# Four graph layers on one core: row sums of the adjacency matrix by four column quarters of TensorE, and one chain of roots for twelve tiles

## The chip, the cores and the metric

The kernel runs on one core of a Trainium2 chip. The time is device microseconds of that core for one launch; lower is better. The times given are medians of several executions; the profile is that of one more execution.

## What is computed

Four graph layers follow each other on x (2708 x 512) with one adjacency matrix adj (2708 x 2708, some 0.6% of it filled, and a filled diagonal). The first one, cut from the reference:

```python
h = jnp.maximum(_layernorm(x, axis=-1), 0.0)
deg = jnp.sum(adj_matrix, axis=1)
dinv = (deg + 1.0) ** (-0.5)
aug = dinv[:, None] * (adj_matrix + jnp.eye(n)) * dinv[None, :]
x = x + jax.nn.relu(aug @ h @ weight)
```

The second layer uses (deg + 1e-8) ** -0.5 without the added unit matrix, the third again the form of the first, and the fourth an attention over the neighbours. So before the first product can be scaled, the row sums deg of all of adj that belong to a tile of h must be known, with the root of deg + 1 and the mean and variance of the tile's rows of x.

## The kernel before, in words

The matrix arrives transposed, so that deg is a sum over columns' partitions: a sum down the 128 partitions of each block. Its rows and columns are cut into four quarters of 677. Each quarter has five full tiles of 128 rows; what is left (37 rows of each quarter) is gathered in two tail tiles, so there are NT = 22 tiles, of which NF = 20 are full. A block is yb[j, q, u]: the 5 x 128 full rows of quarter j by one half (u, 339 columns) of quarter q. It is 128 x 1695 f32 in SBUF, 847.5 KB. yt holds the tail rows.

The products adj @ h are done by a Winograd-like scheme on two levels: outer_product and multiply take sums and differences of blocks (DVE additions of 128 x 1695) and of halves of h, so that seven products do the work of eight. multiply (L446) runs products pa, pb, pc, pd of five matmuls each (L454) into PSUM banks; inner_x (L405) makes the sums s1 to s4 of h, and inner_y (L421, additions L428 to L431) those of the blocks.

The first layer (first_aggregate, L585) does this while the degrees are made. Its order:

- Two tail loads (L592), then four pieces (q, u) in degrees (L281). Each loads two blocks of the lower half of the matrix (L286, into one of three places, `early`) and two of the upper half that are kept for the product (L289), adds the first two on DVE (L290), adds the unit matrix's diagonal to the kept block (add_loops, L389), and sums columns on PE with column_sums (L254): the stationary operand is one column of ones, and the moving one 128 x 339 of a block, so that one partition of PSUM takes the sums (15 matmuls, L258, and two for the tails in tail_sums_of, L251 and L252). ACT copies the row of sums out (L261).
- After the second piece of a quarter, quarter_h (L263) cuts the two rows of sums into tiles' columns and first_h (L324) turns them into columns: a matmul each (L330) with the 128 numbers as stationary operand and a single one as moving operand. Then come the roots: rsqrt (L179) is a square root on ACT, a reciprocal and four small DVE instructions that refine it, once for the degree and once for the variance; then ACT normalizes five tiles (L211).
- h of quarters 0 and 1 (XA, XB) now stands, and the first product p1 runs for both halves u. Meanwhile DVE makes sums of blocks for later products (third_sums L622, second_sums L629) that GpSimd writes to DRAM (keep_o, L376).
- The degrees of quarters 2 and 3 come in other_degrees (L298), from block sums that the product makes anyway, before each half of product 7. Their tiles' x is loaded late (L653), and their statistics (first_stats, L657) and roots follow: a chain of roots for quarter 2, one for quarter 3, and one for each of the two tail tiles (tail_degrees, L314).
- Then h of the quarters 2 and 3 is subtracted (by_halves, L662; minus_sum, L399) and the product of the next kind begins. other_roots (L340) makes the second layer's roots five tiles at a time.

The order of the instructions on each engine isn't that of the source alone: a list scheduler of the framework interleaves them, within the dependencies, when the program is built. Each engine then takes its own in order. SP issues the loads in order and waits, with all behind it, where a place isn't free. PSUM has five banks for the products (`ps_agg`), two for `ps_out`, one for `ps_sm`.

Of the kernel before, what the change touches and what calls it, by code (L numbers as in the profile page):

```python
# [8 lines left out]
FP = mybir.dt.float32  # L9
AF = mybir.ActivationFunctionType  # L10
ALU = mybir.AluOpType
# [26 lines left out]
def gnn_kernel(  # L38
# [40 lines left out]
        nc.vector.tensor_add(again_ident, again_ident, ident[:, k * G : (k + 1) * G])  # L79
    ones = const.tile([P, P], FP, name="ones")  # L80
    nc.vector.memset(ones, 1.0)
    bab = const.tile([P, 2], FP, name="bab")
    nc.gpsimd.dma_start(bab[:, 0:1], ba.partition_broadcast(P))
    nc.gpsimd.dma_start(bab[:, 1:2], bb.partition_broadcast(P))
# [52 lines left out]
    def take(places):  # L137

        places.append(places.pop(0))
        return places[-1]  # L140
# [13 lines left out]
    def repeat(g, n):  # L154

        while n < P:
            nc.vector.tensor_copy(g[..., n : 2 * n], g[..., 0:n])
            n *= 2
# [17 lines left out]
        return [g[:, c] for c in range(len(cs))]  # L176


    def rsqrt(o, v, n):  # L179

        s = small.tile([P, KT], FP, tag="rs", name="rs")
        nc.scalar.activation(s[:, :n], v, AF.Sqrt)
        nc.vector.reciprocal(o, s[:, :n])
        q = small.tile([P, KT], FP, tag="rq", name="rq")
        nc.vector.tensor_mul(q[:, :n], o, o)
        nc.vector.tensor_mul(q[:, :n], q[:, :n], v)
        nc.vector.tensor_scalar(q[:, :n], q[:, :n], -0.5, 1.5, ALU.mult, ALU.add)
        nc.vector.tensor_mul(o, o, q[:, :n])
# [4 lines left out]
        nc.vector.bn_aggr(mv, st)  # L193

    def rstd_of(mv, n):
        v = small.tile([P, KT], FP, tag="rv", name="rv")
        nc.vector.tensor_scalar(v[:, :n], mv[:, :n, 1], LN_EPS, None, ALU.add)
        rstd = small.tile([P, KT], FP, tag="rstd", name="rstd")
        rsqrt(rstd[:, :n], v[:, :n], n)
        return rstd  # L200

    def shift_of(mv, scale, n):

        b = small.tile([P, KT], FP, tag="sh", name="sh")
        nc.vector.scalar_tensor_tensor(
            b[:, :n], mv[:, :n, 0], -1.0, scale[:, :n], ALU.mult, ALU.mult
        )
        return b
# [25 lines left out]
            stats(h[:, t, :], mv0[:, t, :])  # L234


    left = ends[0:1, 4 * BLK : ENDS]
    acct = left[:, 2 * W : 2 * W + NQ * (R0 + R1)].rearrange("p (q r) -> p q r", q=NQ)
    parts = {(0, u): left[:, u * W : (u + 1) * W] for u in range(U)}
    parts[1, 0] = between[0:1, 3 * BLK : 3 * BLK + W]  # L240

    def load_tails(q, u, tl=None):
        if tl is None:
# [2 lines left out]
            nc.sync.dma_start(tl[:, s, :], yt[s, :, q, u])  # L246
        return tl

    def tail_sums_of(ps, tls):

        nc.tensor.matmul(ps[0:1], ones[:, 0:1], tls[0], start=True, stop=False)  # L251
        nc.tensor.matmul(ps[0:1], ones[:G, 0:1], tls[1], start=False, stop=False)  # L252

    def column_sums(ps, blocks, to):  # L254

        last = KT * len(blocks) - 1
        for n in range(last + 1):
            nc.tensor.matmul(  # L258
                ps[0:1], ones[:, 0:1], blocks[n // KT][:, n % KT, :], start=False, stop=n == last
            )  # L260
        nc.scalar.copy(to, ps[0:1])  # L261

    def quarter_h(q, two):  # L263

        nc.vector.tensor_copy(acct[:, q, :], two[1][:, KT * P - W : Q - W])
        across = small.tile([1, P], FP, tag="across", name="across", bufs=1)
        k = W // P
        nc.vector.tensor_copy(across[:, 0 : W - k * P], two[0][:, k * P : W])
        nc.vector.tensor_copy(across[:, W - k * P : P], two[1][:, 0 : (k + 1) * P - W])

        def columns(t):
            o = (t % KT) * P
            if t % KT == k:
                return across
            return two[0][:, o : o + P] if t % KT < k else two[1][:, o - W : o - W + P]

        first_h(list(range(q * KT, (q + 1) * KT)), columns)

    y11 = {}

    def degrees(q, u, ps):  # L281


        two = [take(early) for _ in range(2)]
        for k in range(2):
            nc.sync.dma_start(two[k], yb[2 + k, q, u])  # L286
        for j in (q, 1 - q):
            y11[j, q, u] = blk = free.pop(0)
            nc.sync.dma_start(blk, yb[j, q, u])  # L289
        nc.vector.tensor_add(two[0], two[0], two[1])  # L290
        add_loops(y11[q, q, u], u, 1)
        column_sums(ps, [two[0], y11[q, q, u], y11[1 - q, q, u]], parts[0, u])

    def tail_place(b, u):

        return agg[:, 1, 1, :, b, u * W : (u + 1) * W]

    def other_degrees(u, ys):  # L298

        if u == 0:  # L300
            parts[1, 1] = upool.tile([P, W], FP, tag="s", name="row")[0:1]
        for b, blocks in ((0, (ys[1], ys[2])), (1, (ys[7],))):
            ps = ps_out.tile([P, W], FP, tag="out", name="dg_ps")
            tl = tail_place(b, u)
            tail_sums_of(ps, (tl[:, 0], tl[:G, 1]))
            column_sums(ps, blocks, parts[b, u])
        if u < U - 1:
            return
        for b in range(2):
            quarter_h(2 + b, [parts[b, v] for v in range(U)])  # L310
        tail_degrees(NF)
        tail_degrees(NF + 1)

    def tail_degrees(t):  # L314
        o, m = (0, R0) if t == NF else (R0 - PAD, R1P)
        g = small.tile([1, P], FP, tag="dt", name="dt", bufs=1)
        nc.vector.tensor_scalar(
            g[:, 0 : NQ * m].rearrange("p (q r) -> p q r", q=NQ), acct[:, :, o : o + m],
            1.0, None, ALU.add,
        )  # L320
        repeat(g, NQ * m)
        first_h([t], lambda t: g)

    def first_h(ts, columns):  # L324

        n, t0 = len(ts), ts[0]
        span = slice(t0, t0 + n)
        pd = ps_sm.tile([P, KT], FP, tag="sm", name="pd")
        for s, t in enumerate(ts):
            nc.tensor.matmul(pd[:, s : s + 1], columns(t), ones[0:1, 0:1], start=True, stop=True)  # L330
        nc.vector.tensor_copy(deg[:, span], pd[:, :n])
        rsqrt(dinv[:, span], deg[:, span], n)
        mv = mv0[:, span, :]
        rstd = rstd_of(mv, n)
        nc.vector.tensor_mul(rstd[:, :n], rstd[:, :n], dinv[:, span])
        sh = shift_of(mv, rstd, n)
        for s, t in enumerate(ts):
            normalized(t, h[:, t, :], rstd[:, s : s + 1], sh[:, s : s + 1])

    def other_roots():  # L340

        nc.vector.tensor_scalar(deg, deg, 1.0, 1e-8, ALU.subtract, ALU.add)
        for t in range(0, NT, KT):
            n = min(KT, NT - t)
            rsqrt(dis[:, t : t + n], deg[:, t : t + n], n)

# [236 lines left out]
    def first_aggregate(epilogue):  # L585
# [2 lines left out]
        free += more  # L588
        spare = [block(later_h, k * BLK) for k in range(3)]
        tls = [tpool.tile([P, KT, W], FP, tag="t", name=f"tails{s}") for s in range(2)]  # L590
        for s in range(2):
            nc.sync.dma_start(  # L592
                tls[s][:, 0 : 2 * U], yt[s, :, 0:2].rearrange("p q u w -> p (q u) w")
            )
        pieces = [(q, u) for q in range(2) for u in range(U)]
        ps = {a: ps_agg.tile([P, W], FP, tag="agg", name="dg_ps") for a in pieces}
        for q, u in pieces:
            tail_sums_of(ps[q, u], (tls[0][:, q * U + u], tls[1][:G, q * U + u]))
        for q, u in pieces:
            degrees(q, u, ps[q, u])  # L600
            ts = range(q * KT, (q + 1) * KT)
            if u == 0:
                first_x(ts)
                first_stats(ts)
            else:
                quarter_h(q, [parts[0, v] for v in range(U)])
            if (q, u) == (1, 0):
                ys = inner_y([y11[a, b, u] for a, b in QUAD], u, 0, own_t3)
        blks = {u: [y11[a, b, u] for a, b in QUAD] for u in range(U)}
# [4 lines left out]
        p1, p7 = (0, 0, "as it is"), (1, 1, "as it is")  # L614
        for u in range(U):
            for b in range(2):
                load_tails(2 + b, u, tail_place(b, u))
        xs_ = inner_x(XA)
        multiply(xs_, ys, 0, [p1])
        ys = inner_y(blks[1], 1, 0, own_t3)  # L620
# [341 lines left out]
    def attention(t, columns):  # L962
        xt = load_x(t, xs)
        y = load_x(t, xbs)
        nc.scalar.activation(xt, xt, AF.Copy, bias=0.5)
        sm = ps_sm.tile([P, KT], FP, tag="sm", name="pse")
        nc.tensor.matmul(sm[:, 0:1], columns(t), ones[:, 0:1], start=True, stop=True)
        pE, _ = project(wsa_sb, t)
        g = small.tile([P, 1], FP, tag="ge", name="ge")
        nc.vector.tensor_add(g, sm[:, 0:1], eps[:, t : t + 1])  # L970
        nc.vector.reciprocal(g, g)
        nc.vector.tensor_mul(g, g, ga[:, t, 0:1])
        nc.vector.scalar_tensor_tensor(y, pE, g, y, ALU.mult, ALU.add)
        nc.scalar.activation(y, y, AF.Tanh, scale=0.5)
        nc.vector.scalar_tensor_tensor(xt, y, 0.5, xt, ALU.mult, ALU.add)
        for o, n, to in place(t):
            nc.gpsimd.dma_start(out[to : to + n, :], xt[o : o + n, :])
# [140 lines left out]
```

## Time and profile before

| | |
|---|---|
| median of 3 runs | 2152.46 us (2147.79 to 2152.94) |
| the profiled execution, its own time | 2149.36 us |
| its span, first to last instruction | 2147.6 us |
| mean granted TensorE clock | 0.994 |
| PE busy | 2100.2 us (98%), 7270 matmul passes |
| DVE busy | 1448.8 us (67%), 2573 instructions |
| ACT, POOL busy | 385.8 us (18%), 171.1 us (8%) |
| moved by DMA | 359.10 MB, mean 167 GB/s |

Each f32 matmul stands as two records (passes) in the trace, each with its weight load. A busy PE is a PE that has a matmul in its pipe, not one at its peak. The whole span is:

```profile
PE   8999979999999999999999999999999999999998
DVE  4799857567666867777576869968537755666512
DMA  8894596445554444654453656554542233233212
```

One digit is the busy share, in tenths, of a fortieth of the span (53.7 us). The parts that the change touches lie in the first four digits.

The sums of columns have two neighbours in the trace. First, the single column of ones: weight loads of 128 x 1 take 79 to 128 ns, matmuls of 128 x 339 446 to 451 ns from start to end. Second, the transposing matmuls (L330): 245 ns, with weight loads of 181 to 187 ns, 44 in number (22 tiles, two passes).

### The profile page before, as it was taken

The numbers are of one execution on the slowest core, as the hardware profiler recorded it, in microseconds if no ns is written. First come the engines' busy times: TensorE is split into PE (matmuls) and PEld (weight loads), VectorE is DVE, ScalarE is ACT, GpSimd is POOL, SyncE is SP. The second block draws the span as 40 slices with busy tenths as digits, with TensorE's granted clock in tenths as the row PEclk, the third lists the DMA queues.
The fourth block names the chain that finished last, engine by engine and source line by source line (L and its number), as shares of the span: only waits on it lengthen the run. The fifth ranks groups of instructions, "written<-read, shape, count | busy, mean of one in ns | idle before, by whom it ended". The sixth has DMA issues, their size and how long they took to land.

```text
span 2147.6 us, 19913 instructions
## 1 busy us (share of the span) xinstructions
PE 2100.2 (98%) x7270; PEld 1288.8 (60%) x7270; DVE 1448.8 (67%) x2573; ACT 385.8 (18%) x765; POOL 171.1 (8%) x314
## 2 busy tenths in 40 slices
PE   8999979999999999999999999999999999999998
PEld 2556646556666645566664546666677666666664
DVE  4799857567666867777576869968537755666512
ACT  1121000222000010100001121000116534444401
POOL 0000010211000020200001130000001000000001
PEclk9999989999999999999999999999999999999999
DMA  8894596445554444654453656554542233233212
GB/s 334 322 357 166 181 304 200 163 148 201 177 169 166 154 152 153 227 171 156 162 176 127 220 196 205 173 162 158 192 163 75 97 101 101 94 101 100 80 41 65
DMA packets 79201, 359.10 MB, mean 167 GB/s; under 512 B 10540, under 2 KB 14892, under 8 KB 79104
## 3 DMA queue, kind: packets, MB, share of 16 engines
q1 hardware_dynamic: 51584, 252.02, 34.4%
q0 software_dynamic: 27520, 105.82, 14.6%
q8 instruction: 57, 0.93, 0.2%
q14 instruction: 40, 0.33, 0.0%
HBM read 295.65 MB, written 62.15 MB: 167 GB/s over the span
## 4 chain that ended last, share of the span: by engine, by line
PE 52%; issue 33%; DVE 7%; DMA 6%; POOL 2%; ACT 1%; POOLq 0%; SPq 0%; DVEq 0%; ACTq 0%
PE pa L454 10%; PE pd L454 9%; PE pc L454 9%; PE po L734 6%; PE pb L454 5%; PE pe L1025 4%; PE pg L873 3%; PE pt L505 2%; PE dg_ps L258 2%; DMA ends<-xs 1%; POOL ends L741 1%; DMA obuf<-in_yb_dram 1%; DMA obuf<-osumt 1%; PE pt L510 1%; DVE ends L826 1%
## 5 line engine op out<-in xcount | busy, mean ns | idle before, releaser
L1025 PE MATMUL pe<-obuf,h 128*128 128x339 f32 x1280 | 372.9, 448 | 0.0
L454 PE MATMUL pa<-obuf,h 128*128 128x339 f32 x1050 | 321.4, 450 | 3.1 <-ACT h L211 1.6
L1025 PEld LDWEIGHTS pe<-obuf,h 128*128 128x128 f32 x1280 | 240.9, 189 | 126.6 <-issue 10.0
L734 PE MATMUL po<-ends,agg 128*128 128x512 f32 x640 | 281.4, 596 | 1.8 <-ACT ends L754 1.5
L454 PEld LDWEIGHTS pa<-obuf,h 128*128 128x128 f32 x1050 | 198.6, 190 | 108.8 <-issue 7.5
L734 PEld LDWEIGHTS po<-ends,agg 128*128 128x128 f32 x640 | 119.6, 190 | 144.6 <-issue 137.7
L454 PE MATMUL pd<-obuf,s 128*128 128x339 f32 x550 | 168.6, 453 | 14.5 <-DVE agg L471 14.4
L946 ACT ACTIVATE e<-r,nsr 128x339 f32<-128x339 f32 x352 | 170.8, 566 | 28.0 <-DVE obuf L950 11.6
L454 PE MATMUL pc<-t,h 128*128 128x339 f32 x560 | 169.4, 448 | 2.9 <-DVE u L492 2.9
L454 PE MATMUL pb<-t,s 128*128 128x339 f32 x560 | 169.9, 448 | 0.2 <-DVE s L399 0.2
L454 PE MATMUL pd<-t,s 128*128 128x339 f32 x560 | 169.2, 448 | 0.0
L482 ACT COPY v<-pa 128x339 f32<-128x339 f32 x56 | 24.6, 440 | 746.3 <-PE pa L454 709.9
L454 PEld LDWEIGHTS pd<-obuf,s 128*128 128x128 f32 x550 | 104.9, 191 | 69.9 <-DVE agg L471 17.0
L454 PEld LDWEIGHTS pc<-t,h 128*128 128x128 f32 x560 | 105.8, 189 | 57.9 <-DVE u L492 4.5
L454 PEld LDWEIGHTS pd<-t,s 128*128 128x128 f32 x560 | 105.9, 189 | 54.3 <-issue 0.5
L454 PEld LDWEIGHTS pb<-t,s 128*128 128x128 f32 x560 | 105.4, 189 | 54.5 <-DVE s L399 0.7
L454 PE MATMUL pc<-obuf,s 128*128 128x339 f32 x450 | 136.1, 448 | 0.0
L454 PEld LDWEIGHTS pc<-obuf,s 128*128 128x128 f32 x450 | 85.2, 189 | 43.7 <-issue 0.5
L429 DVE TENSOR_TENSOR t<-obuf,t 128x1695 f32<-128x1695 f32 x55 | 105.5, 1918 | 0.0
L430 DVE TENSOR_TENSOR t<-obuf,t 128x1695 f32<-128x1695 f32 x53 | 101.6, 1917 | 0.0
L760 POOL DMA_DIRECT2D xs<-ends x66 | 35.9, 543 | 818.3 <-DVE ends L759 757.1
L1042 DVE COPY agg<-pe 128x339 f32<-128x339 f32 x16 | 7.5, 506 | 138.2 <-PE pe L510 138.2
(232 smaller groups left out, 2321.5 us busy)
## 6 DMA issues: line engine op xcount, KB each, us to landing
obuf<-in_yb_dram SPq DMA_DIRECT2D x131, 847.5 KB, 4.5
obuf<-osumt SPq DMA_DIRECT2D x100, 847.5 KB, 4.5
osumt<-obuf POOLq DMA_DIRECT2D x23, 847.5 KB, 9.1
xs<-ends POOLq DMA_DIRECT2D x66, 256.0 KB, 2.3
ends<-xs POOLq DMA_DIRECT2D x66, 256.0 KB, 3.4
obuf<-in_yt_dram SPq DMA_DIRECT2D x32, 339.0 KB, 3.6
agg<-in_yb_dram SPq DMA_DIRECT2D x12, 847.5 KB, 11.3
ends<-in_yb_dram SPq DMA_DIRECT2D x11, 847.5 KB, 8.5
```

The lines of the kernel that those rows point to most:

```text
L258: nc.tensor.matmul(ps[0:1], ones[:, 0:1], blocks[n // KT][:, n % KT, :], start=False, stop=n == last)
L429: nc.vector.tensor_add(t2, o22, t1)
L430: at_t4.append(nc.vector.tensor_add(t4, o21, t2).ins)
L454: nc.tensor.matmul(ps, xs_[q][:, k, :], ys[q][:, k, :], start=start and k == 0, stop=k == KT - 1, skip_group_check=not start,)
L482: nc.scalar.copy(v, pa)
L505: nc.tensor.matmul(ps[c], h[:, NF, c * P : (c + 1) * P], tl[:, 0, :], start=start, stop=False)
L510: nc.tensor.matmul(ps[c], h[g, NF + 1, c * P : (c + 1) * P], tl[g, 1, :], start=False, stop=True)
L734: nc.tensor.matmul(po, cs[c], w_sb[:, c, :], start=(c == 0), stop=(c == NC - 1))
L760: nc.gpsimd.dma_start(xs[t], xt)
L873: nc.tensor.matmul(pk, cs[c], wg_sb[:, c, k, :], start=(c == 0), stop=(c == NC - 1))
L946: nc.scalar.activation(e[:, k], row, AF.Exp, bias=nsr[:, t, s : s + 1], scale=1.0)
L1025: nc.tensor.matmul(pe[c], h[:, t, c * P : (c + 1) * P], a, start=(t == 0), stop=False)
```

## The change

The column sums are made in four column quarters of PE: matmul n of a piece uses columns 32 (n mod 4) and on, with a stationary operand `first` of 128 x 32 (a first column of ones, the rest zero), and writes its own 32 partitions of the bank. So four partial sums stand in partitions 0, 32, 64 and 96, with zeros between. ACT copies all 128 partitions, and the transposing matmul, with 128 ones as moving operand, adds the four. The tails count as two more moving operands, and the second one is filled up with zeros to 128 partitions.

degrees sums all four blocks straight: the DVE addition of two blocks is gone, five more matmuls a piece come in. The diagonal is added to the block after it has been summed, so the degree gets its 1 in first_h. The places for blocks that are only summed are six instead of three (`spare + early`). The loads of tails are one call each (load_rows), the second of 32 rows.

other_degrees collects the columns of quarters 2 and 3 and of both tails and calls first_h once, for twelve tiles: one pair of roots instead of four. other_roots makes one root of 22 columns instead of five. Scratch for roots of more than five columns is hd and eps, which the kernel has for the last layer.

In the built program the scheduler places some things anew. On PE, the five first matmuls of p1 (pa, quarter 0) stand among the sums of piece (1,0), and the transposing matmuls of the twelve tiles stand between the fifth and the sixth of the second half of product 7's seven groups (pa, pb, pa, pc, pd, then pc, pd). On DVE, the chain of roots of the twelve tiles is spread between the additions of blocks L428 to L431, L471 and L703. After about 200 us of the program the order is the same on PE, DVE and SP.

```diff
+    first = const.tile([P, 32], FP, name="first")
+    nc.vector.memset(first, 0.0)
+    nc.vector.memset(first[:, 0:1], 1.0)
...
+    def small_cols(tag, n):
+
+        if n <= KT:
+            return small.tile([P, KT], FP, tag=tag, name=tag)
+        k = ("rs", "rq", "rv", "rstd", "sh").index(tag)
+        return hd[:, :, k] if k < 4 else eps
+
     def rsqrt(o, v, n):
 
-        s = small.tile([P, KT], FP, tag="rs", name="rs")
+        s = small_cols("rs", n)
...
-    def tail_sums_of(ps, tls):
-
-        nc.tensor.matmul(ps[0:1], ones[:, 0:1], tls[0], start=True, stop=False)
-        nc.tensor.matmul(ps[0:1], ones[:G, 0:1], tls[1], start=False, stop=False)
-
-    def column_sums(ps, blocks, to):
-
-        last = KT * len(blocks) - 1
-        for n in range(last + 1):
-            nc.tensor.matmul(
-                ps[0:1], ones[:, 0:1], blocks[n // KT][:, n % KT, :], start=False, stop=n == last
-            )
-        nc.scalar.copy(to, ps[0:1])
...
+    def load_rows(a, b, rows):
+
+        nc.gpsimd.memset(b, 0.0)
+        nc.sync.dma_start(a, rows[0])
+        nc.sync.dma_start(b[:G], rows[1, :G])
+
+    def column_sums(ps, tls, blocks, to):
+
+
+        ops = tls + [blk[:, k, :] for blk in blocks for k in range(KT)]
+        for n, y in enumerate(ops):
+            g = slice(n % 4 * 32, n % 4 * 32 + 32)
+            nc.tensor.matmul(ps[g], first, y, start=n < 4, stop=n >= len(ops) - 4)
+        nc.scalar.copy(to, ps)
...
-    def degrees(q, u, ps):
-
-
-        two = [take(early) for _ in range(2)]
+    def degrees(q, u, ps, tls, places):
+
+        blocks = [take(places) for _ in range(2)]
         for k in range(2):
-            nc.sync.dma_start(two[k], yb[2 + k, q, u])
+            nc.sync.dma_start(blocks[k], yb[2 + k, q, u])
         for j in (q, 1 - q):
             y11[j, q, u] = blk = free.pop(0)
             nc.sync.dma_start(blk, yb[j, q, u])
-        nc.vector.tensor_add(two[0], two[0], two[1])
+            blocks.append(blk)
+        column_sums(ps, tls, blocks, parts[0, u])
         add_loops(y11[q, q, u], u, 1)
-        column_sums(ps, [two[0], y11[q, q, u], y11[1 - q, q, u]], parts[0, u])
...
         for b in range(2):
-            quarter_h(2 + b, [parts[b, v] for v in range(U)])
-        tail_degrees(NF)
-        tail_degrees(NF + 1)
...
+            columns.update(quarter_columns(2 + b, [parts[b, v] for v in range(U)]))
+        columns.update((t, tail_columns(t)) for t in (NF, NF + 1))
+        first_h(columns, NF - half)
...
+    def first_h(columns, looped):
+
+        ts = list(columns)
         n, t0 = len(ts), ts[0]
         span = slice(t0, t0 + n)
-        pd = ps_sm.tile([P, KT], FP, tag="sm", name="pd")
+        pd = ps_sm.tile([P, NT], FP, tag="sm", name="pd")
         for s, t in enumerate(ts):
-            nc.tensor.matmul(pd[:, s : s + 1], columns(t), ones[0:1, 0:1], start=True, stop=True)
-        nc.vector.tensor_copy(deg[:, span], pd[:, :n])
+            nc.tensor.matmul(
+                pd[:, s : s + 1], columns[t], ones[:, 0:1], start=True, stop=True
+            )
+        if looped:
+            nc.vector.tensor_copy(deg[:, t0 : t0 + looped], pd[:, :looped])
+        if looped < n:
+            nc.vector.tensor_scalar(
+                deg[:, t0 + looped : t0 + n], pd[:, looped:n], 1.0, None, ALU.add
+            )
...
-        for t in range(0, NT, KT):
-            n = min(KT, NT - t)
-            rsqrt(dis[:, t : t + n], deg[:, t : t + n], n)
+        rsqrt(dis, deg, NT)
...
+        places = spare + early
         for q, u in pieces:
-            tail_sums_of(ps[q, u], (tls[0][:, q * U + u], tls[1][:G, q * U + u]))
-        for q, u in pieces:
-            degrees(q, u, ps[q, u])
+            ps = ps_agg.tile([P, W], FP, tag="agg", name="dg_ps")
+            degrees(q, u, ps, [tl[:, q * U + u] for tl in tls], places)
             ts = range(q * KT, (q + 1) * KT)
             if u == 0:
                 first_x(ts)
                 first_stats(ts)
             else:
-                quarter_h(q, [parts[0, v] for v in range(U)])
+                first_h(quarter_columns(q, [parts[0, v] for v in range(U)]), 0)
```

## The prediction, made before the changed kernel ran

> **What bounds the kernel now.** I read the page, then the busy time in stretches of the first 300 us (the change touches nothing later), then the column sums' tile, then the timeline and the chain of waits where they stand. Table by stretch (PE, weight loads, DVE, ACT, POOL busy us; granted clock; DMA share; GB/s):
> ```profile
> 10.00:15.00 5.00, 5.00 (x9) 0.33 (x8) 1.79 (x1) 0.00 (x0) 0.00 (x0) 1.00 1.02 427
> ...
> 20.00:25.00 5.00, 5.00 (x18) 1.42 (x17) 3.50 (x9) 0.00 (x0) 0.00 (x0) 1.00 0.97 366
> 25.00:30.00 5.00, 2.73 (x12) 1.02 (x11) 2.80 (x7) 0.43 (x1) 0.00 (x0) 1.00 1.03 430
> 30.00:35.00 5.00, 5.00 (x13) 1.26 (x12) 0.65 (x3) 0.00 (x0) 0.00 (x0) 0.66 0.60 231
> ...
> 75.00:80.00 5.00, 5.00 (x19) 3.28 (x18) 4.43 (x4) 0.00 (x0) 0.00 (x0) 1.00 0.00 1
> ...
> 130.00:140.00 10.00, 10.00 (x35) 4.58 (x34) 10.00 (x9) 2.45 (x1) 0.82 (x2) 1.00 1.02 418
> ```
> In the first 65 us PE, the DMA engines and DVE take turns: transfers run at about 425 GB/s where nothing holds them, and dip (231) where SP waits for one of three places for blocks. From 92 to 150 us PE, DMA and DVE are all full. That matters most: there, time taken off PE alone buys nothing.
>
> The column sums, by tile:
> ```profile
> L258 PE MATMUL dg_ps<-obuf,ones x90: 446/447/451, 20.5 to 142.9; 128*1 128x339 f32 x90
> L258 PE MATMUL dg_ps<-agg,ones x50: 446/448/773, 15.3 to 112.3; 128*1 128x339 f32 x50
> L258 PE MATMUL dg_ps<-ends,ones x40: 446/447/450, 60.0 to 147.1; 128*1 128x339 f32 x40
> ```
> Each f32 matmul is two records: 180 records, 90 matmuls. 447 ns is latency; the pace is 2.86 us for 10 records, 0.286 us a pass, 0.572 us a matmul.
>
> PE's timeline around the end of the stage, and around the next product that DVE feeds:
> ```profile
> 60.01 3.02 PE L258 MATMUL dg_ps<-ends,ones 128*1 128x339 f32 x10
> ...
> 67.93 4.75 PE L454 MATMUL pa<-obuf,h 128*128 128x339 f32 x10 [1.61 <-ACT h L211]
> ...
> 175.45 1.98 PE L454 MATMUL pa<-obuf,h 128*128 128x339 f32 x6 [0.94 <-ACT v L482]
> 177.27 3.02 PE L454 MATMUL pb<-t,s 128*128 128x339 f32 x10
> ```
> So 67.93 us (first product of both quarters) and 177.27 us (first product after the second roots) are the two posts against which I measure. From 177 to 290 us PE is without a gap, and its order and DVE's after about 205 us are the same in both kernels: what is gained at 177.27 is gained at the end. The 12.4 us wait near 290 us is a chain of loads and accumulating transfers started by earlier PE events; it shifts with them.
>
> **Stage 1, to 67.93 us: removed, added, moved.** Removed: four block additions on DVE (L290, 1.93 us each) that PE waited for. Added: 5 more matmuls a piece, 22 instead of 17, on four column quarters. No row shows column quarters. The nearest row is four row groups in tail_products:
> ```profile
> 310.09 0.85 PE L510 MATMUL pt<-obuf,h 32*128 32x339 f32 x8
> 310.87 2.55 PE L505 MATMUL pt<-obuf,h 128*128 128x339 f32 x8
> ```
> Four f32 matmuls (8 passes) take 310.09 to 310.87, 0.78 us instead of 2.29. The Trainium skill, "TensorE: Matmul & The Clock Gate", Part 3, gives three column tiles 2.38 times one; as an estimate that is 0.72 us for three. By the row a piece is 5.5 rounds x 0.78 = 4.3 us, by the page 22/3 x 0.72 = 5.3 us; before 17 x 0.572 = 9.7 us. Bounds: 0.57 us a round (perfect), 2.29 (no overlap). I take 0.78, or 1.3 at the half clock that idle PE gets (0.66 in the 30:35 row): 7.2 us a piece. A rule that speaks against: "TensorEngine Tiling (Array Packing)", Key Properties, says that changing the tiling mode drains the array. The row prices it: from the last full-array start to the row groups' first, and back, the step is about 0.09 us longer than 0.286. Some 26 switches are 2.3 us if all lay on the path; most lie in waits, so I count none here.
>
> Either price is below a piece's loads: four blocks of 847.5 KB, 3.47 MB, 8.2 us at 425 GB/s. So the transfers bound. To the last block of piece (1,1) there are 13.9 MB of blocks, 2.6 of x, 0.9 of tails, 17.4 MB. Before moved 2.2 MB by 10 us (rows 209 and 222 GB/s); the same start, then 425 GB/s, gives 10 + 15.2/0.425 = 45.8 us. Six places instead of three mean that SP no longer waits while the queue empties: only the seventh and eighth block reuse a place, whose sums are done near 20 us while the queue is filled to beyond 35. The zeroing of the second tail block on POOL (128x1356; a 128x128 memset takes 0.20 us, so 0.2 to 2.1 us) holds SP with x and the later blocks behind it until about 5 us, under 8 us of queued blocks: nothing; uncovered, 2 us. The four smaller memsets stand ahead of POOL's first write, near 87 us: nothing. The eight block loads behind piece (1,1) on SP go partly to its first places, read by about 43 us, before the queue runs empty. ACT's copies grow from 1 to 128 partitions: 0.43 us, as L482's 128x339 (0.44); the transposing matmuls likewise: nothing.
>
> Then: sums of the last two blocks, 2.5 rounds, 2.0 to 3.3 us: 48.5 us. DVE is later. Piece (0,1) has landed by 10 + (9.1 - 2.2)/0.425 = 26.3 us and is summed by 28.3; copies, transposing products, the activation table's load (1.28 us) and the roots, some 5 us, let quarter 0 be normalized from 33.4 to 37.0. In PE's new order five matmuls of the first product stand among the sums of (1,0) and wait for this, and ten sums behind them: PE is at 38.6 us when the block that DVE's diagonal additions wait for has been read (before, they went ahead of the sums). Queued behind these on DVE: four additions of 1.85 us and five tiles of statistics (0.78 each), the next diagonal and the copies: 38.6 + 0.65 + 7.4 + 3.9 + 1.3 = 51.9 us. I take 51.9. From the last such copy (63.67) to the product were 4.26 us. So 56.1 instead of 67.93: **-11.8 us**. Bounds: -16 (DMA and PE alone), -7 (everything at half clock, 380 GB/s).
>
> **Stage 2, the sums of the other quarters.** They take PE 5.8, 2.95 and, with the transposing matmuls, 12.5 us (106.90 to 112.70, 116.33 to 119.28, 136.19 to 148.70), 21 us; after, 2 x 5 rounds x 0.78, plus the 12 small products and switches, about 10. **PE gets 11 us, and I credit none of them.** Transfers saturated from 92 us and DVE full from 80 start with the first products, so they move by 11.8 us and no more: x's second half lands at 147.4 - 11.8 = 135.6 us, and the last statistics, with some 0.7 us of root instructions gone from between, end at 152.5 - 12.5 = 140.0. PE will stand instead, near 138 to 142 us, as the twelve columns' products are queued on PE ahead of the last two products and wait for DVE's copies.
>
> **Stage 3, one chain of roots.** Removed: of four chains three, of other_roots four of five; about 40 instructions of 0.07 to 0.15 us, 4 to 5 us of DVE in all, half before 177. Added: the chain is spread between large additions in DVE's order, and no tile is normalized before all twelve are ready. Walking that order from 140.0: the sum u2, the first addition (1.85), u3, degree copies: 143.3; one subtraction and the first reciprocal 143.9; second addition, three small, third addition 147.8; subtraction 148.4; fourth 150.3; subtraction 150.9; L703's addition 152.9; six small ones, 153.7. Then ACT normalizes twelve at 0.725: five by 157.4, ten by 161.1. L399 on h's first half waits for five (to 158.8), the second for ten (162.5); L696 2.75 and s2 0.75: 166.0 us. Before:
> ```profile
> 159.75 1.49 DVE L399 SCALAR_TENSOR_TENSOR h<-h 128x1280 f32<-128x1280 f32 x1
> ...
> 168.76 2.82 DVE L696 TENSOR_TENSOR h<-h 128x2560 f32<-128x2560 f32 x1
> ...
> 172.66 1.49 DVE L399 SCALAR_TENSOR_TENSOR h<-h 128x1280 f32<-128x1280 f32 x1
> ...
> 175.96 0.83 DVE L399 SCALAR_TENSOR_TENSOR s<-h,s 128x640 f32<-128x640 f32 x1
> ```
> s2 was there at 176.8: -10.8. But PE has idled some 10 us, and its first five matmuls go at half clock (5.7 instead of 2.9 us), ACT's copy v and three more behind them: pb at about 167.0. **Sum at the second post: 167.0 - 177.3 = -10.3 us.** Bounds of this stage alone: 3 us better (the wait for twelve hidden by earlier statistics), 5 worse (x late).
>
> **The number.** The profiled execution took 2149.4 us (span 2147.6): 2139.1. The median of the runs, 2152.5, is 3.1 above it: 2142.2. The runs spread over 5 us, so I say 2141.
>
> **Rivals.**
> 1. The PE time of stage 2 is gained too, because x lands or statistics end earlier than the shift. For: DVE has 3 us of small waits in 143 to 158. Against: the 130:140 row with DMA 1.02 and DVE 10.00. About -12 - 11 = -23: 2129. Chance 0.14.
> 2. The quarters do not overlap: the change doesn't do what it says. 22 x 0.572 = 12.6 us a piece, from 12.4 us (tails landed): 62.8 against 63.0 us at the end of the sums. Stage 3, counted from there as above, lands at 177 to 179: 0 to +2, 2153. Against it: the row groups' 0.78. Chance 0.12.
> 3. Slower: each change of quarter waits for the previous matmul's full latency, two passes of 447 ns, 0.89 us a matmul. Four pieces end at 12.4 + 88 x 0.89 = 91 us, +28, and the later 38 matmuls cost 34 instead of 21: together about +35, 2187. The point that decides is 0.575 us a matmul, (63.0 - 12.4)/88. Against it: passes on full arrays and on row groups both overlap their latency. Chance 0.08.
>
> **How the numbers follow.** The likeliest case, 0.66, gives 2141, its own range 2134 to 2148. 0.3% of 2152, 6.5 us, is about what a measurement here can tell from no change. Faster: 0.60 of the likeliest case and rival 1, 0.74; within: 0.06 and most of rival 2, 0.16; slower: rival 3 and the rest of rival 2, 0.10. The range 2130 to 2152 leaves out rival 3, half of rival 2 and a part of rival 1.
>
> **What would show it.** Stage 1: no dip in GB/s before 45 us, the first product of both quarters at 54 to 58 us; starts of four column matmuls a few ns apart, and rounds of 0.6 to 1.3 us. Stage 2: PE idle for several us between 130 and 145. Stage 3: normalization of twelve tiles in one stretch of 8.7 us, beginning about 13 us after the last statistics; pb at 164 to 169. I am wrong if a column round takes 2.3 us, if transfers stall in stage 1 for another reason, or if PE has no gap in stage 2.

## The result, and the profile after

The changed kernel takes 2145.70 us (median of 17 runs, 2139.07 to 2151.76) where the kernel before takes 2149.66 us (17 runs, 2147.79 to 2152.94). The ratio is 0.9977, with a 95% interval of 0.9968 to 0.9987: about 4 us, 0.2%, faster. The prediction was 2141 us, 11.5 us below its median of before; the sign and the range held, and some two thirds of the forecast gain did not come. The profiled execution of the changed kernel took 2147.35 us, with a span of 2145.6 us: 2.0 us less than the profiled one before.

Its table by stretch (columns as before: PE, weight loads, DVE, ACT, POOL busy us; granted clock; DMA share; GB/s):

```profile
20.00:25.00 5.00, 5.00 (x44) 2.31 (x37) 1.59 (x5) 0.44 (x1) 0.00 (x0) 1.00 1.03 422
...
30.00:35.00 5.00, 3.01 (x26) 1.24 (x18) 1.93 (x16) 2.37 (x5) 0.00 (x0) 1.00 1.02 417
...
75.00:80.00 5.00, 5.00 (x19) 3.27 (x19) 5.00 (x7) 0.44 (x1) 1.08 (x2) 1.00 0.44 174
...
110.00:120.00 10.00, 8.37 (x30) 5.28 (x29) 9.81 (x13) 0.00 (x0) 1.87 (x4) 1.00 1.00 401
...
140.00:150.00 10.00, 6.58 (x30) 4.73 (x29) 9.73 (x32) 0.45 (x2) 0.55 (x1) 0.80 0.95 346
```

The dip at 30 to 35 us (231 GB/s before) is gone. PE takes 44 passes in the five microseconds from 20 where it took 18. After 110 us PE is no longer always busy, while DMA and DVE stay full up to 150: PE has the lead, and the other two set the pace.

The column sums, by tile (x90 passes; their ns, shortest, median and longest; first and last start):

```profile
L275 PE MATMUL dg_ps<-obuf,first x90: 446/448/773, 21.5 to 124.1; 128*32 128x339 f32 x90
```

PE's timeline in stage 1, from the first sums to the first post:

```profile
17.57 1.36 PE L275 MATMUL dg_ps<-tails,first 128*32 128x339 f32 x3 [17.57 <-DMA tails<-in_yt_dram]
...
19.29 2.98 PE L275 MATMUL dg_ps<-h,first 128*32 128x339 f32 x16
...
40.17 1.91 PE L275 MATMUL dg_ps<-obuf,first 128*32 128x339 f32 x20
...
57.31 4.81 PE L475 MATMUL pa<-obuf,h 128*128 128x339 f32 x10 [2.24 <-ACT h L221]
```

By the tile's row, one pass still lasts 0.45 us, but four quarters run at once. The 20 passes at 40.17 are ten matmuls, two and a half rounds: (1.91 - 0.45) / 2.5 = 0.58 us a round, the price of a single matmul before (0.572). At half clock, at 19.29, two rounds take 2.98 - 0.77 us, 1.1 us each (here the clock is read from the passes, 0.77 us instead of 0.45: the clock column still says 1.00). The first post is at 57.31 us instead of 67.93: -10.6.

PE around the second post, first the line of before for product 7's fourth group, then the changed kernel:

```profile
160.06 3.02 PE L454 MATMUL pc<-ends,s 128*128 128x339 f32 x10
...
135.59 3.02 PE L475 MATMUL pc<-ends,s 128*128 128x339 f32 x10
...
144.62 0.38 PE L346 MATMUL pd<-ones,across 128*128 128x1 f32 x2 [1.78 <-DVE across L286]
...
147.21 0.59 PE L346 MATMUL pd<-ones,dt 128*128 128x1 f32 x2 [1.54 <-DVE dt L160]
147.66 5.69 PE L475 MATMUL pc<-t,h 128*128 128x339 f32 x10
...
164.75 5.69 PE L475 MATMUL pa<-obuf,h 128*128 128x339 f32 x10 [8.53 <-DVE h L420]
...
172.79 3.02 PE L475 MATMUL pb<-t,s 128*128 128x339 f32 x10
```

Product 7's fourth group stands 24.5 us earlier; yet pb is at 172.79 instead of 177.27, only -4.5. Between, PE waits 3.3 us for DVE's copies and 8.53 us for h, and twice five matmuls take 5.69 us instead of 3.02: half clock (0.50 granted in the 160:170 row of this execution). DVE and ACT in the same stretch show what PE waits for; the square brackets end with what DVE itself waited for:

```profile
109.83 1.93 DVE L644 TENSOR_TENSOR obuf<-obuf,h 128x1695 f32<-128x1695 f32 x1 [3.60 <-DMA obuf<-in_yb_dram]
...
139.23 0.69 DVE L202 BATCH_NORM_STATS2 st<-h 128x6 f32<-128x512 f32 x1 [0.89 <-DMA h<-in_x_dram]
...
150.62 1.91 DVE L452 TENSOR_TENSOR ends<-obuf,ends 128x1695 f32<-128x1695 f32 x1
...
153.39 0.51 DVE L492 TENSOR_TENSOR agg<-pc,u 128x339 f32<-128x339 f32 x1 [0.77 <-PE pc L475]
...
153.91 1.92 DVE L451 TENSOR_TENSOR t<-obuf,t 128x1695 f32<-128x1695 f32 x1
...
159.33 0.18 DVE L215 SCALAR_TENSOR_TENSOR eps<-mv,hd 128x12 f32<-128x12 f32 x1
```

ACT's normalization, released by the last of these lines:

```profile
159.54 8.56 ACT L221 ACTIVATE h<-h,eps,hd 128x512 f32<-128x512 f32 x12 [2.27 <-DVE eps L215]
```

Statistics end at 144.4 us. The chain of small instructions on 12 columns is then spread between five additions of 1.9 us, of which two are shown, and two subtractions (L492) that wait 0.77 and 0.33 us for the product at half clock and the one behind it. Its last one, eps, is at 159.33, and only then does ACT normalize all twelve tiles. After 177 us PE's order is the same as before; its shift then lies between -5.1 and -0.8 us. It is -2.0 at the end of this execution and -4.0 between the medians.

### The profile page after: what moved, and what is told of

Same layout as the page of the kernel before. It is cut to its first block, busy times and chain, and to the rows that moved or that the text cites. A ratio compares the mean times of both kernels' runs of the same rounds, so it can differ in the third digit from the quotient of the medians.

```text
span 2145.6 us, 19944 instructions
## 1 busy us (share of the span) xinstructions
PE 2068.6 (96%) x7310; PEld 1289.0 (60%) x7310; DVE 1438.6 (67%) x2513; ACT 384.7 (18%) x755; POOL 173.7 (8%) x319
## 4 chain that ended last, share of the span: by engine, by line
PE 62%; issue 20%; DMA 8%; DVE 7%; POOL 2%; ACT 1%; SPq 0%; POOLq 0%; DVEq 0%; ACTq 0%
PE pa L475 13%; PE pc L475 12%; PE pd L475 12%; PE po L754 7%; PE pb L475 6%; PE pe L1045 4%; PE pt L526 3%; PE pg L893 3%; DMA obuf<-in_yb_dram 2%; DMA h<-in_x_dram 1%; PE pt L531 1%; DVE ends L846 1%; POOL ends L761 1%; DMA ends<-xs 1%; DMA osumt<-obuf 1%
## 5 line engine op out<-in xcount | busy, mean ns | idle before, releaser
L475 PE MATMUL pd<-obuf,s 128*128 128x339 f32 x550 | 169.0, 454 | 13.3 <-DVE agg L492 13.3
L475 PE MATMUL pc<-t,h 128*128 128x339 f32 x560 | 173.8, 457 | 4.4 <-DVE u L513 4.4
L449 DVE TENSOR_TENSOR t<-obuf 128x1695 f32<-128x1695 f32 x49 | 94.1, 1920 | 9.8 <-DMA obuf<-in_yb_dram 6.6
```

Of the source, the lines that this page charges most:

```text
L449: nc.vector.tensor_add(t1, o12, o11)
L475: nc.tensor.matmul(ps, xs_[q][:, k, :], ys[q][:, k, :], start=start and k == 0, stop=k == KT - 1, skip_group_check=not start,)
```

## The experiments

Theory A, formed from these lines: PE's lead is lost in stage 3, because the one chain of roots lies between block additions with nothing left for PE to do, and then PE, idle, starts at half clock. Rival B: the transfers set stage 2 and 3; x and the blocks land late, the statistics end late, and the place of the chain is beside the point. No experiment leaves work of the reference out. Medians are of the runs compared; each ratio is to the kernel before, run on the same chip. The posts are each those of one profiled execution. From the second post to the end these twelve executions take 1967 to 1978 us, so a few us of a median need not come from the posts.

| kernel | median us (runs) | ratio, 95% interval | first post | second post |
|---|---|---|---|---|
| before, with the first four / next four / last two | 2149.36 (19) / 2150.76 (27) / 2150.76 (17) | | 67.93 | 177.27 |
| changed | 2145.70 (17) | 0.9977, 0.9968 to 0.9987 | 57.31 | 172.79 |
| three chains | 2137.28 (6) | 0.9947, 0.9929 to 0.9964 | 56.83 | 161.49 |
| one chain ahead of the additions | 2138.68 (5) | 0.9947, 0.9931 to 0.9963 | 59.78 | 166.72 |
| before, with one chain | 2147.58 (14) | 0.9995, 0.9985 to 1.0005 | 68.92 | 175.76 |
| one sum after another | 2157.11 (4) | 1.0041, 1.0025 to 1.0058 | 78.64 | 183.22 |
| three places | 2145.39 (11) | 0.9972, 0.9963 to 0.9982 | 58.37 | 174.39 |
| three chains ahead of the additions | 2137.37 (6) | 0.9939, 0.9926 to 0.9953 | 59.84 | 164.91 |
| diagonal before the sums | 2144.64 (15) | 0.9975, 0.9966 to 0.9985 | 57.12 | 171.38 |
| PE kept warm | 2141.84 (6) | 0.9961, 0.9947 to 0.9975 | 58.02 | 171.90 |
| tails first | 2143.30 (13) | 0.9968, 0.9960 to 0.9976 | 58.55 | 172.63 |
| tails first, three chains | 2134.07 (5) | 0.9926, 0.9911 to 0.9940 | 55.96 | 161.39 |

**Three chains.** The roots of quarter 2, of quarter 3 and of the two tails apart, the sums as in the changed kernel:

```
-        columns = {}
         for b in range(2):
-            columns.update(quarter_columns(2 + b, [parts[b, v] for v in range(U)]))
-        columns.update((t, tail_columns(t)) for t in (NF, NF + 1))
-        first_h(columns, NF - half)
+            first_h(quarter_columns(2 + b, [parts[b, v] for v in range(U)]), KT)
+        first_h({t: tail_columns(t) for t in (NF, NF + 1)}, 0)
```

> The changed kernel, but other_degrees calls first_h three times (quarter 2, quarter 3, both tails) instead of once for twelve tiles. Theory A (the long chain of roots, spread between block additions on DVE, holds the normalization back to 159.5 us and so eats PE's lead): quarter 2 is normalized before 152 us, pb of the first product after the roots starts at 164 to 168 us instead of 172.8, and the time is 5 to 9 us under the changed kernel's, about 2138. Rival B (late x and its statistics, which end at 144 us, set the start whatever the chain's form): pb at 171 to 174 us, the time within 2 us of the changed kernel's 2145.7.

Measured: 2137.28 us, 8 us below the changed kernel, the intervals apart. ACT's normalization:

```profile
144.83 3.63 ACT L221 ACTIVATE h<-h,sh,rstd 128x512 f32<-128x512 f32 x5 [0.44 <-DVE sh L215]
148.89 3.63 ACT L221 ACTIVATE h<-h,sh,rstd 128x512 f32<-128x512 f32 x5 [0.24 <-DVE sh L215]
```

and PE's first product after it, to the second post:

```profile
154.98 3.02 PE L473 MATMUL pa<-obuf,h 128*128 128x339 f32 x10
...
161.49 3.02 PE L473 MATMUL pb<-t,s 128*128 128x339 f32 x10
```

Ten tiles are normalized by 152.5 us, before the changed kernel has begun (159.54), and PE goes from pd to pa at 154.98 without the wait of 8.53 us. The blocks that DVE had at 109.83 came 2.2 us earlier here (107.68), and the statistics end at 141.6 instead of 144.4: a part, but far from the 11.3 us at the second post, which came earlier than even A expected. That speaks for A and against B as the main limit. The median gains 8.

**One chain ahead of the additions.** The additions of the next product may only be issued after the chain's last shift, `at_sh[-1]` (the list in which the kernel now notes each shift is left out here):

```
-            multiply(xs_, inner_y(t2, u, 0, own_t3), u, [(0, 1, "added")])
+            if u == 1:
+                with tc.issue_after(at_sh[-1]):
+                    ys = inner_y(t2, u, 0, own_t3)
+            else:
+                ys = inner_y(t2, u, 0, own_t3)
+            multiply(xs_, ys, u, [(0, 1, "added")])
```

> The changed kernel with its one chain of twelve tiles, but the four block additions of the next product are held behind the chain's last instruction on DVE. Theory A: the shift of the twelve tiles is ready near 151.5 us instead of 159.5, the additions fill DVE's waits for ACT's normalization, pb at 164 to 167 us, the time 6 to 9 us under the changed kernel's, about 2138. Rival B: nothing moves by more than 2 us. A third case: the additions, now late, hold pb or pd themselves; then pb at 168 to 172 us.

Measured: 2138.68 us, though its first post came 2.5 us later than the changed kernel's. From the end of the statistics (147.1) to the end of eps, the last of the chain on DVE, it takes 8.6 us, not 15.1 (eps is still 4 us later than expected, 2.5 of it from the first post):

```profile
155.46 0.18 DVE L218 SCALAR_TENSOR_TENSOR eps<-mv,hd 128x12 f32<-128x12 f32 x1
```

So most of the cost is not that twelve tiles are in one chain, but where it stands. From the first post to the second it is 115.5 us in the changed kernel, 106.9 here and 104.7 with three chains: the place is worth 8.5 of the 10.8 us, and 2.3 are left for the wait for all twelve. With three chains ahead of the additions, the two edits do not add up:

> Both earlier edits together: roots for quarter 2, quarter 3 and the tails apart, and the next product's block additions held behind the second of these chains on DVE. Split chains alone put pb at 161.5 us with PE nearly without a gap from 146 us on, so theory A expects little more: pb at 159 to 163 us, the time within 3 us of the split chains' 2137. A fall of over 4 us would mean that DVE's additions still held something there.

Measured: 2137.37 us. pb is at 164.91, beyond the 159 to 163 expected and 3.4 us later than with three chains alone, of which 3.0 is its later first post. In the medians, either edit alone gives as much as both.

**The kernel before with one chain** (twelve tiles and 22 roots at once, nothing of the sums changed; the cut shows the one call, not the scratch and the helpers that follow from it):

```
...
         for b in range(2):
-            quarter_h(2 + b, [parts[b, v] for v in range(U)])
-        tail_degrees(NF)
-        tail_degrees(NF + 1)
+            cols.update(quarter_columns(2 + b, [parts[b, v] for v in range(U)]))
+        cols.update((t, tail_columns(t)) for t in (NF, NF + 1))
+        first_h(cols)
...
```

> The kernel before with the one chain alone: sums in one column as before, but one chain of roots for twelve tiles and one for other_roots. In this build the scheduler puts the chain ahead of the block additions on DVE. Theory A (not the chain's length but its place costs): within 4 us of the kernel before, 2146 to 2154, pb at 174 to 180 us. Rival C (waiting for all twelve tiles costs by itself, as no tile is normalized before the last degree): 4 to 9 us slower than before, pb at 181 us or later.

Measured: no difference (0.9985 to 1.0005). Its eps ends 7.5 us after the statistics (161.5 against 154.0), with the chain ahead of all but one addition, and PE, held back by the sums in single file, still has product 7 to do. It arrives at pb when s is all but there, a wait of 0.20 us in PE's timeline (this profiled execution was the slowest of the 14, at 2155.18 us; what it lost lies behind the second post):

```profile
175.76 3.13 PE L461 MATMUL pb<-t,s 128*128 128x339 f32 x10 [0.20 <-DVE s L406]
```

The fewer instructions on DVE show no gain by themselves there: PE is all but without a gap. The change's gain is the sums'; its chain only decides how much of it survives.

**One sum after another.** The stationary operand has 128 columns (one of ones, the rest zero), so that every sum takes the whole array:

```
-    first = const.tile([P, 32], FP, name="first")
+    first = const.tile([P, P], FP, name="first")
...
-            g = slice(n % 4 * 32, n % 4 * 32 + 32)
-            nc.tensor.matmul(ps[g], first, y, start=n < 4, stop=n >= len(ops) - 4)
+            nc.tensor.matmul(ps, first, y, start=n == 0, stop=n == len(ops) - 1)
```

> The changed kernel with its sums on the full array: a stationary operand of 128 columns, the first ones, the rest zero, so no two sums overlap; all else as changed. If the loads bound stage 1 and the quarters only keep PE under them: a piece takes 22 x 0.572 = 12.6 us on PE, more than its 8.2 us of loads, from 17.6 us on; the first product of both quarters at 70 to 75 us instead of 57.3, the time 8 to 16 us over the changed kernel's (2154 to 2162), slower than before. If PE is not near the bound of stage 1 at all: within 4 us of the changed kernel.

Measured: 2157.11 us, slower than before (1.0025 to 1.0058) and 11.4 above the changed kernel. The sums are PE's queue here, until 76.7 us; five matmuls take 2.86 us from start to start, the last block of piece (1,1), at 50.04 in the changed kernel, is read at 67.41, and the first post comes at 78.64, later than expected:

```profile
67.41 3.02 PE L274 MATMUL dg_ps<-ends,first 128*128 128x339 f32 x10
```

The overlap of the four quarters is thus worth what the change gains and more; without it the 20 added matmuls cost more than DVE's four additions saved.

**Three places** instead of six for the blocks that are only summed:

```
-        places = spare + early
+        places = early
```

> The changed kernel with the three places of before for blocks that are only summed, instead of six. If SP's waits for places emptied the queue (the prediction's reading of stage 1): piece (1,0)'s blocks are issued only after the sums of piece (0,0), near 24 us, with gaps in the transfers; the first product of both quarters at 60 to 66 us instead of 57.3, the time 1 to 6 us over the changed kernel's. If the number of places does not matter once PE reads blocks quickly: the product within 1.5 us of 57.3, the same time.

Measured: 2145.39 us, the changed kernel's time. SP waits for places (its two loads from 5.12 us on take 15.5 us), but behind a filled queue: the DMA share is 0.99 or more in every row from 10 to 50 us. The row that dipped, here and, below it, with one sum after another, which has six places and slow sums:

```profile
30.00:35.00 5.00, 3.94 (x18) 1.71 (x16) 1.94 (x16) 2.56 (x5) 0.00 (x0) 0.65 1.02 422
...
30.00:35.00 5.00, 5.00 (x19) 3.35 (x18) 0.20 (x1) 0.44 (x1) 0.00 (x0) 1.00 1.01 412
```

So neither cause of the dip stands alone. Three places are enough if the sums are quick, and six carry slow sums past 35 us; there the queue runs empty later (5 GB/s in the 55:60 row).

**Diagonal before the sums**, as it was:

```
+        add_loops(y11[q, q, u], u, 1)
         column_sums(ps, tls, blocks, parts[0, u])
-        add_loops(y11[q, q, u], u, 1)
```

(with the degree's 1 then in the block, for quarters 0 and 1).

> The changed kernel with the diagonal added to the block before it is summed, as in the kernel before (the degrees of quarters 0 and 1 then hold their 1 already). The prediction let DVE wait for PE's sums there, and took that wait with DVE's additions behind it as the bound of stage 1. If so: the additions of piece (1,0) begin 1 to 2 us earlier than 41.5 and the first product of both quarters at 55 to 56.5 us. If transfers bound (the last block landed near 50): 57 us or later, as PE now waits for DVE at the last block. Time within 3 us of the changed kernel's.

Measured: 2144.64 us, no difference between the medians. DVE no longer waits for PE's sums of piece (1,0), but the sums of (1,1) wait for DVE, and the first post is at 57.12:

```profile
50.65 0.88 PE L275 MATMUL dg_ps<-obuf,first 128*32 128x339 f32 x4 [1.88 <-DVE obuf L410]
```

**PE kept warm.** 32 matmuls of constants, with a result that nobody reads, after the last matmul of product 7's second half (`at_mm`, the list of the products' matmuls, is left out here):

```
+        with tc.issue_after(at_mm[-1]):
+            warm = ps_out.tile([P, W], FP, tag="out", name="warm")
+            for _ in range(32):
+                nc.tensor.matmul(warm[:, 0:P], ident, ones, start=True, stop=True)
```

> The changed kernel with 32 matmuls of 128 columns of constants put on PE between the last product before the second roots and the first one after them, so that PE is not idle there; their result is not used. If the half clock after the 8.5 us of idle PE costs what the trace shows: the five matmuls that took 5.69 us at 164.75 take 2.9, pb starts near 170 instead of 172.8, and the time is 2 to 3 us under the changed kernel's. If the clock is held by something else, or the constants do not count as work: no change.

Measured: 2141.84 us, 3.9 below the changed kernel, with intervals that just overlap. PE's timeline:

```profile
156.20 7.31 PE L686 MATMUL warm<-ones,ident 128*128 128x128 f32 x64
164.91 3.12 PE L476 MATMUL pa<-obuf,h 128*128 128x339 f32 x10 [1.40 <-DVE h L420]
...
174.86 3.02 PE L476 MATMUL pc<-ends,s 128*128 128x339 f32 x10
```

The wait for h is the same, but behind it five matmuls take 3.12 us instead of 5.69. Counted from each kernel's first post, pc, by which PE has done the same matmuls in both, stands at +116.8 instead of +119.5. Of these 2.6 us, 0.5 were there by the end of the wait; from pa to pc it is 9.95 us instead of 12.04. A's second part holds, in one execution: the half clock after the wait is 2.1 us of the path.

**Tails first.** The second tail load waits for a memset of 1.25 us on GpSimd, and the scheduler put both tail loads behind four blocks on SP; here DVE, idle then, writes the zeros:

```
-    def load_rows(a, b, rows):
+    def load_rows(a, b, rows, zeroed_by=nc.gpsimd):
...
-        nc.gpsimd.memset(b, 0.0)
+        zeroed_by.memset(b, 0.0)
...
-            yt[:, :, 0:2].rearrange("s p q u w -> s p (q u) w"),
+            yt[:, :, 0:2].rearrange("s p q u w -> s p (q u) w"), nc.vector,
```

> The second block of tails is zeroed by DVE, idle then, instead of GpSimd (1.25 us at 2.89 us in the changed kernel). So the tails' loads are queued on SP behind one block instead of four, and PE's first sums should begin well before the 17.57 us of the changed kernel (before the change: 5.1). Transfers decide: the last blocks land near 50 us as in the changed kernel, the first product of both quarters starts at 56 to 58.5 us, the time is within 2 us of the changed kernel's 2145.7. Late sums decide: PE, 5 to 8 us earlier, reads the first blocks earlier, the diagonals on DVE move with it, and the product starts near 53 us, time 2142 or below.

Measured: 2143.30 us, 2.4 below the changed kernel and not told apart from it, as the intervals overlap. The sums begin 8.6 us earlier, and the first post is 1.2 us later (the second line shown is ten matmuls of piece (1,0)):

```profile
8.95 2.15 PE L275 MATMUL dg_ps<-tails,first 128*32 128x339 f32 x4 [8.95 <-DMA tails<-in_yt_dram]
...
41.41 1.91 PE L275 MATMUL dg_ps<-obuf,first 128*32 128x339 f32 x20
...
58.55 5.70 PE L475 MATMUL pa<-obuf,h 128*128 128x339 f32 x10 [2.24 <-ACT h L221]
```

The twenty passes at 41.41 release the diagonal on DVE. In eight kernels with this order (all but that with the diagonal first and that with one sum after another) they start between 38.83 and 42.71 us, and the first post follows 17.13 to 17.15 us later in every one. So stage 1 ends on that DVE chain, and neither "transfers" nor "late sums" of the expectation had the cause. What the start goes with is PE's granted clock between 33 and 42 us: 1.00 where it is at 38.83 or 40.17; 0.84, 0.81 and 0.71 at 39.69, 40.87 and 41.23; 0.62 at 41.41, 42.64 and 42.71. The clearest pair is this kernel and the next one: their PE lines agree within 0.02 us from 26.14 to the first matmul of p1, at 34.17 and 34.19, and then the passes stand at 41.41 here and there at

```profile
38.83 1.91 PE L275 MATMUL dg_ps<-obuf,first 128*32 128x339 f32 x20
```

At the same clock of 1.00, earlier tails are worth 1.3 us (38.83 against 40.17, one execution each); here they were lost to the clock again.

The same with three chains:

> The same, with the roots in three chains (quarter 2, quarter 3, both tails), which alone took 2137.3. Transfers decide: 2136 to 2139, and the first product after the second layer's roots near 161.5 us as in the kernel with three chains. Late sums decide: both some 3 us earlier, 2134 and 158.

Measured: 2134.07 us, 0.7% below the kernel before and the fastest of all. Clock 1.00 between 33 and 42, first post 55.96; but pb is at 161.39, as with three chains alone, so the second edit's 3 us between the medians have no cause in this trace (the two profiled executions differ by 3.0 us too, 2.9 of it behind the second post), and the two intervals overlap. What is shown is that three chains beat both kernels.

## Why the prediction was right and wrong

**The bound and stage 1** were right in the main: -10.6 for -11.8. The column round was taken at 0.78 us, by the row groups; the Trainium skill, "TensorE: Matmul & The Clock Gate", Part 3, with 2.38 times one for three column tiles, makes it 0.72 for three, as an estimate. Measured is 0.58 for four, better than both, and it mattered little, as the prediction said: DVE ends the stage. The transfers took longer than the sum had it (the last block of piece (1,1) is read as it lands, at 50.04 us, not 45.8), which cost nothing: DVE took the copy of its sums only at 53.16, 1.3 us after ACT had made it. DVE's chain, from PE's sums of the block to be read to the first product, was put at 56.1 - 38.6 = 17.5 us and is 17.14. The mis-sized term is the start, 38.6, which was 40.17. The prediction had put the zeroing of the second tail block at nothing; the tails landed at 17.57, and with the tails first the start is 38.83 at full clock, so they explain 1.3 of the 1.6 us. The clock, which the sum took as given, moves it by up to 2.6 more. The reason given for the missing dip, six places, is only one of two: three do as well.

**Stage 2** held in its main point: none of PE's time was gained at once, PE's lead grew to 24.5 us and it stood still afterwards. The step that failed is "they move by 11.8 us and no more". They moved by less: DVE had y22's blocks at 109.83 instead of 116.55 (-6.7), x's second half at 139.23 instead of 147.42 (-8.2), and the statistics ended at 144.4 where 140.0 was predicted. That is 4.4 us, 1.2 of it from stage 1 and 3.2 here. The lines of before:

```profile
114.15 1.92 DVE L431 TENSOR_TENSOR ends<-agg,ends 128x1695 f32<-128x1695 f32 x1
116.55 4.00 DVE L624 TENSOR_TENSOR obuf<-obuf,h 128x1695 f32<-128x1695 f32 x2 [0.48 <-DMA obuf<-in_yb_dram]
...
147.42 0.69 DVE L192 BATCH_NORM_STATS2 st<-h 128x6 f32<-128x512 f32 x1 [0.86 <-DMA h<-in_x_dram]
```

and the same addition ahead of y22's blocks in the changed kernel:

```profile
103.61 1.92 DVE L452 TENSOR_TENSOR ends<-agg,ends 128x1695 f32<-128x1695 f32 x1
```

DVE itself kept the whole shift up to there (-10.5), and then waited for the blocks. The table rows from the start to y22's first block, before and changed, say why the blocks came later than that:

```profile
0.00:116.55 116.55, 105.55 (x337) 45.34 (x338) 71.88 (x120) 14.70 (x26) 6.17 (x16) 0.97 0.87 333
0.00:109.83 109.83, 81.84 (x409) 45.33 (x410) 66.02 (x121) 15.73 (x28) 8.71 (x21) 0.98 0.92 350
```

By then 38.8 and 38.4 MB have been moved, in 101 us of full DMA work in both (0.87 x 116.55, 0.92 x 109.83). With the same work ahead of them, the blocks can come earlier only by idle time of the DMA engines that goes away. It fell from some 15 to some 9 us; what is left lies in the first 10 us and near 75 us (1 and 174 GB/s in the 75:80 rows). So the loads do not simply start with the first products: they queue behind the transfers of stage 1, which the change leaves as they are. This is read from one trace of each kernel; no experiment moved x or these loads.

**Stage 3**: statistics to eps was put at 13.7 us and took 15.1. The order of the additions was walked rightly, but the walk gave DVE no waits for PE: it waited 0.27 us for the transposing product, 0.77 for pc, which came at half clock (5.69 us), and 0.33 for pd behind it, 1.4 us in all. Half clock was counted behind the wait for h, not ahead of it. From the end of eps to pb, 13.3 were predicted and 13.3 measured, the half clock of pa with it.

The sum: 1.2 + 3.2 + 1.4 = 5.8 us, which is 172.8 - 167.0: pb, forecast at 164 to 169, came at 172.79. That the -4.5 reached the end as -4.0 between the medians is in part luck, as the rest of the path varies by more. Luck helped the number too: the 3.1 us that were added because the median of three runs lay above the profiled execution are not there in 17 runs (2149.66), and without them the forecast would have been 2139.

**The rivals.** That PE's time in stage 2 is gained too (2129) did not happen, but not for the reason given alone: with three chains 11 us more were there at the second post, at a median of 2137, with blocks only 2 us earlier. The prediction priced "no tile is normalized before all twelve are ready" into its sum, but didn't ask what the old chains would have given behind the new sums. The other two are answered by the round of 0.58 us; had the quarters not overlapped, the time would have been not the 2153 predicted but 2157. Rival 3's own terms, +28 and 34 - 21, come to +41 and not +35; it makes no difference here.

## What to carry to other kernels

When one engine gets far ahead, work that was hidden behind it comes onto the path: a chain of small instructions must then stand ahead of the big ones on its engine, or be split so that the first part of its result is used early. Pooling small operations saves instructions, but delays the first result to the last input; it cost nothing here as long as the waiting engine had other work. Where transfers fill most of a stretch, take their busy time as fixed and ask only how much idle time is left to lose. A lead that ends in an idle PE also costs its clock (5.69 us instead of 3.12 for five matmuls after 8.5 us of waiting), so price the first matmuls after a gap at both clocks.

## What was not expected of the hardware

- Four column quarters of f32 matmuls (32 columns, 339 moving) cost no more than one: 0.58 us a round of four against 0.572 for one, and 1.1 at half clock. At 40.17 us in the changed kernel the passes of the four quarters start 6 to 7 ns apart.
- The half clock is a matter of chance as well: the same instructions between 33 and 42 us ran at a granted clock of 1.00 in two kernels, 0.62 in three and in between in three more, and the first post moved by up to 2.6 us with it. The Trainium skill, "TensorE: Matmul & The Clock Gate", Part 1, says that the window over which busy time is judged runs freely, so that the point of change varies from run to run; that fits, but no run here shows the window itself. The same part puts the ramp at under 1% of a typical kernel's span. That is true of the gap ahead of pa (2.1 us of 2145), which is still half of the whole gain.
- Matmuls of two constant tiles, of 128 columns, kept the clock up in the one execution that had them: 64 passes, 7.31 us, a wait of 1.40, and the next five f32 matmuls took 3.12 us.
